# A graph transformer kernel on one core: seven edge buffers of seven slots with even chunks, four node blocks ahead of the type sort, single blocks and a third product tile at the end of the first layer

## Chip, cores and metric

The kernel runs on one core of a Trainium2 chip. The metric is the device time of one execution in microseconds (us), lower is better. The core has a matrix engine (TensorE, PE in the profile), a vector engine (VectorE, DVE), a scalar engine (ScalarE, ACT) and GpSimd (POOL), which here issues every indirect transfer, that is, every gather and scatter with addresses from a list. SyncE (SP) issues plain transfers; 16 DMA engines move the data.

## The reference

6250 nodes of 128 features, 100,000 edges sorted by destination, 16 node types and 32 edge types, 8 heads of 16, everything in float32. Two layers, then a linear layer and a layer norm:

```python
def gt_layer(x, ntype, etype, src, dst, Wk, Wq, Wv, Wa, Watt, Wmsg, pri, skip, g, b):
    k = typed_linear(x, ntype, Wk).reshape(n, H, HS)    # a weight matrix per node type
    q = typed_linear(x, ntype, Wq).reshape(n, H, HS)
    v = typed_linear(x, ntype, Wv).reshape(n, H, HS)
    kT = jnp.einsum('nhd,htdo->nhto', k, Watt)          # every node with every edge type
    vT = jnp.einsum('nhd,htdo->nhto', v, Wmsg)
    kw = kT[src, :, etype]
    m = vT[src, :, etype]
    a = jnp.einsum('ehd,ehd->eh', kw, q[dst]) * pri[:, etype].T / SQRT_D
    att = edge_softmax(a, dst, n)
    msg = (m * att[:, :, None]).reshape(-1, H * HS)
    hag = jax.ops.segment_sum(msg, dst, num_segments=n)
    h = jax.nn.silu(typed_linear(hag, ntype, Wa))
    alpha = jax.nn.sigmoid(skip[ntype])[:, None]
    h = h * alpha + x * (1.0 - alpha)
    return layernorm(h) * g + b
...
return layernorm(x + (layer1(layer0(x)) @ ff_w + ff_b))
```

## The kernel before

**The table.** Each layer first makes, for every node, `kT` and `vT` with all 32 edge types and writes them to memory as a table: a row of 1 KB (128 numbers of K, 128 of V) for each pair of node and edge type. A node's 32 rows are written as two pieces of 16. `table_block` (L337) makes the two pieces of a block of 128 nodes: matmuls of the node's K or V with the block-diagonal edge weights `bdk`, `bdv` (L349) into PSUM tiles `tb`, copies of these (by ScalarE L357, some by the vector engine L355) into a staging tile `st` of 2.1 MB, and then a store: one indirect DMA of GpSimd, L1163 for layer 0 and L1753 for layer 1.

**Start and first table.** `load_first` and its neighbours (L186 to L215, L374 to L385) load the weights. The edge weights come as eight strided transfers each for `Watt` and `Wmsg`, in runs of 64 bytes, into memory set to zero, and `scale_edge_weights` multiplies them by `pri`. Next the nodes are sorted by type: counts by matmul (L442 to L470), a place for each node, and three rounds (L483 to L493) of one-hot matrices and matmuls that turn places into the list `inv`, which says which node stands where. `fetch` (L508) gathers sorted node rows by `inv` (L515), `first0` and `linears0` make K and V of a type's blocks, and the loop at L1176 goes through 49 sorted blocks, two pieces each, 98 in all. Beside it the vector engine sorts the edges' destinations by degree (`ranking`), which decides the order of nodes in the edge stage. In this stretch the engines DVE and POOL run in program order.

**The edge stage** (`edges`, L1302, once a layer). The nodes are sorted by degree into blocks of 128, and each block has as many slots as the largest degree in it: `OWN_SLOTS` = 25, 21, 19, 18, ... slots for four groups of nodes with four node types each, and `MIXED_SLOTS` = 42, 20, 16, 14, 9 for nodes that don't fit. That makes 49 blocks and 819 slots. A slot is one gather of 128 table rows (L1519). The loop (L1485 to L1559) takes a block's slots in chunks of `CH` = 4: for each chunk a buffer `kv` (12 of them), its gathers, the product with the query (L1535) and the reduction to scores (L1541). After each of the three operations stands one `step()`, which advances the closing sequence of the block before (`finished`, L1362) by one step: mask, maximum, exponential, the products of V with the weights chunk by chunk, and the sums over slots. A buffer goes back to the gathers once its V product has been added up. The 42-slot block has 26 slots of its own and 2 more shared by a few nodes (`OWN`, `REST`): seven chunks and one for the rest. Between the chunks `tick` advances other work by a count of slots: the queries of the next superblock, the node chain (`nodes`, L1617: divide, typed linear, silu, mix, norm, and in layer 0 K, V and Q of layer 1), and in layer 0 the table pieces of layer 1 (`pieces_of`, L1765; scatters L1753). In layer 1 the chain ends in the row writes of the output (`put_out`, L1783). `leave` (L1336) counts chunks down and lets each such row write go after `7+2*i` chunks. Instructions recorded by the helper `on` all have line 267.

**The end of a layer.** The superblocks (up to four blocks each) are cut at L1225 to L1239. The last group's are laid out so that its final superblocks hold two blocks each, the last of all with 25 and 21 slots. The first gather of layer 1 waits for every piece of layer 1's table, so the last superblock's node chain and pieces stand between the layers. A product tile `tb` of layer 0's edge stage holds two banks; there are two such tiles, used in turn.

Of the kernel before, what the change touches and what calls it, by code (L numbers as in the profile page):

```python
# [10 lines left out]
F32 = mybir.dt.float32  # L11
BF16 = mybir.dt.bfloat16
# [8 lines left out]
P = 128  # L21

J = 17
# [10 lines left out]
CH = 4  # L34
# [19 lines left out]

def windows_of_types(n, pad, types, width):

    import math  # L60

    low, high = [0], [0]
    for t in range(1, types):
        share = t / types
        mean, dev = pad + n * share, math.sqrt(n * share * (1 - share))
        low.append(max(0, int((mean - 5.0 * dev) // P) * P))
        high.append(int(mean + 5.0 * dev) + 1)
    assert n / types + pad + 5.0 * math.sqrt(n / types) <= width
    return low, high
# [3 lines left out]
def kernel(  # L73
# [53 lines left out]
    LO, HI = windows_of_types(N, NP - N, TY, WIN)  # L127
    WC = max(HI[t] - LO[t] for t in range(TY)) + WIN
    WB = -(-WC // P)

# [40 lines left out]
    wq0 = wts.tile([P, TY, D], F32, name="wq0")  # L171
    wa = wts.tile([P, TY, D], F32, name="wa")

    bdk = wts.tile([P, RT, 2 * HS], F32, name="bdk")
    bdv = wts.tile([P, RT, 2 * HS], F32, name="bdv")
# [10 lines left out]
    def load_edge_weights(l):  # L186
        nc.vector.memset(bdk, 0.0)
        nc.vector.memset(bdv, 0.0)
        for h in range(H):
            s = slice(h * HS, (h + 1) * HS)  # L190
            c = slice((h % 2) * HS, (h % 2 + 1) * HS)
            nc.scalar.dma_start(bdk[s, :, c], Watt[l, h].rearrange("t d o -> d t o"))
            (nc.scalar if l else nc.sync).dma_start(bdv[s, :, c],
                                                    Wmsg[l, h].rearrange("t d o -> d t o"))
        (nc.scalar if l else nc.sync).dma_start(
            prit,
            pri[l].unsqueeze(1).to_broadcast([H, HS, RT]))

    def scale_edge_weights():

        first = nc.vector.tensor_scalar(prit, prit, 1.0 / float(HS) ** 0.5, None, op0=ALU.mult)
        nc.vector.tensor_tensor(bdk, bdk, prit.unsqueeze(2).to_broadcast([P, RT, 2 * HS]),
                                op=ALU.mult)
        return first
# [3 lines left out]
    def load_first():  # L208
        load_typed(wkqv[:, 0], Wk[0])
        load_typed(wkqv[:, 1], Wv[0])  # L210
        load_edge_weights(0)
# [125 lines left out]
    def table_block(pool, ps_pool, kT, vT, i, share, bufs, store, w=1):  # L337


        for tg in range(TG):  # L340
            tt = slice(tg * 16, (tg + 1) * 16)
            st = pool.tile([P, 16, 2 * D], F32, name="st", bufs=bufs)
            for half, (yT, bd) in enumerate(((kT, bdk), (vT, bdv))):
                for hp in range(0, HP, w):
                    pt = ps_pool.tile([P, w, SB * P], F32, name="tb").rearrange(
                        "p b (t c) -> p b t c", t=16)
# [27 lines left out]
    nc.sync.dma_start(ntr, ntype.rearrange("(i p) -> i p", p=P))  # L374
    nc.sync.dma_start(dsti, dst[0:P])
# [3 lines left out]
    nc.sync.dma_start(wq0, Wq[0].rearrange("t d o -> d t o"))  # L379
    nc.sync.dma_start(wa, Wa[0].rearrange("t d o -> d t o"))  # L380
# [3 lines left out]
        engines={mybir.EngineType.DVE, mybir.EngineType.Pool}))  # L384
# [14 lines left out]
    nc.gpsimd.iota(rowi, pattern=[[0, 1]], base=0, channel_multiplier=1)  # L399

# [4 lines left out]
    for t in range(TY):  # L405
        nc.gpsimd.memset(base_t[:, 0, t:t + 1], float(LO[t]))
        nc.gpsimd.memset(base_t[:, 1, t:t + 1], float(HI[t] - LO[t]))
# [34 lines left out]
    ty1 = tp.tile([P, TY, NT], BF16, name="ty1", tag="st", bufs=STB0)  # L442
    nc.vector.tensor_tensor(ty1, ntf.unsqueeze(1).to_broadcast([P, TY, NT]),
                            colf[:, :TY].unsqueeze(2).to_broadcast([P, TY, NT]), op=ALU.is_equal)
    ty1f = ty1.rearrange("p t i -> p (t i)")
    sums_t = tp.tile([P, 4, wide], F32, name="sums_t", tag="st", bufs=STB0)
    cnt_t, run_t, at_t, got_t = (sums_t[:, i] for i in range(4))
    ones = pp.tile([P, P], F32, name="ones")
# [7 lines left out]
    for m, pss in ((ones_b, c_pss), (upto_b, b_pss)):  # L456
        for h, ps in enumerate(pss):
            nc.tensor.matmul(ps[:, :half], m, ty1f[:, h * half:(h + 1) * half],
                             start=True, stop=True)
    nc.vector.tensor_copy(cnt_t[:, :half], c_pss[0][:, :half])  # L460
    nc.vector.tensor_copy(cnt_t[:, half:], c_pss[1][:, :half])
    nc.vector.tensor_tensor_scan(run_t, ones[:, 0:1].to_broadcast([P, wide]), cnt_t, 0.0,
# [4 lines left out]
    nc.vector.tensor_tensor(got_t, at_t, ty1f, op=ALU.mult)  # L467
    place = pp.tile([P, NT], F32, name="place")
# [3 lines left out]
    nc.vector.tensor_copy(placei, place)  # L472
# [7 lines left out]
    row1 = tp.tile([P, NT, P], BF16, name="row1", tag="st", bufs=STB0)  # L480
    col1 = tp.tile([P, NT, 2, NT], BF16, name="col1", tag="st", bufs=STB0)
    inv_ps = pps.tile([P, 2, NT], F32, name="ps")
    for i0 in range(0, NT, 17):  # L483
        sl = slice(i0, min(i0 + 17, NT))
        k = sl.stop - sl.start
        nc.vector.tensor_tensor(col1[:, sl, 1], placeb[:, sl].unsqueeze(2).to_broadcast([P, k, NT]),
                                colb[:, :NT].unsqueeze(1).to_broadcast([P, k, NT]), op=ALU.is_equal)
        nc.vector.tensor_tensor(col1[:, sl, 0], col1[:, sl, 1],
                                colb[:, sl].unsqueeze(2).to_broadcast([P, k, NT]), op=ALU.mult)
        nc.vector.tensor_scalar(col1[:, sl, 1], col1[:, sl, 1], rowf, None, op0=ALU.mult)  # L490
# [1464 lines left out]
```

## Time and profile before

| | us |
|---|---|
| median of 3 runs (2978.79 to 2982.26) | 2979.05 |
| profiled execution, its own time | 2978.13 |
| span of its profile | 2976.3 |
| start, up to the first table write | 53.45 |
| from there to the first gather of layer 0 | 540.3 |
| edges of layer 0, first to last gather | 1164.35 |
| between the layers, to the first gather of layer 1 | 86.77 |
| edges of layer 1, first to last gather | 1090.03 |
| from the last gather to the end | 41.44 |

The prediction quotes rows of the profile. In the rows of the windows view a window comes first, then its length and the busy time of each engine with the number of its instructions in parentheses (PE matmuls, PEld weight loads, DVE, ACT, POOL), the clock granted to TensorE as a share of full speed, the busy share of the 16 DMA engines, and the GB/s that they moved. A row of the groups has line, engine, operation, output<-inputs, count, then busy us and mean ns, then idle time of the engine just before these instructions and what ended most of it. A row of the timeline has start, duration, engine, line, operation, tiles, and in brackets the idle time before it and what ended it: "issue" is time in which the engine waited for nothing that the profile shows.

### The profile page before, as it was taken

What the parts mean: (1) busy time and instruction counts of PE and PEld (TensorE: products, weight loads), DVE (VectorE), ACT (ScalarE), POOL (GpSimd) and SP (SyncE); (2) the same over time, 40 slices, a digit from 0 to 9 for tenths busy, and PEclk for the clock granted to TensorE, in tenths of its full rate; (3) what the DMA queues carried; (4) which work ended last, traced back from release to release, by engine and by line L of the source; (5) the groups of instructions that cost most, each with busy time, mean ns of one, the idle gap of its engine ahead of it and who ended that gap; (6) DMA issues with size and microseconds to landing.
All of it is one profiled execution on the core that took longest, in us unless ns stands there. A gap on an engine that the chain in (4) does not pass through costs nothing. (4 is left out here: it accounts for less than half of the span.)

```text
span 2976.3 us, 21675 instructions
## 1 busy us (share of the span) xinstructions
PE 1670.6 (56%) x5325; PEld 727.2 (24%) x5325; DVE 1895.5 (64%) x4351; ACT 996.6 (33%) x1678; POOL 1975.7 (66%) x2116
## 2 busy tenths in 40 slices
PE   5999978523779887889788995022132113121212
PEld 2444434301323432333233332001011001000001
DVE  7567655357656767677666552576567667766665
ACT  3887533211434444435454562011111111111112
POOL 3332566377777777777777652777777777777773
PEclk9988866655777776787767665555555556555555
DMA  7999999953677678867788895333333333333331
GB/s 210 416 419 419 390 389 396 395 133 104 220 288 271 227 264 300 294 238 278 282 322 297 323 351 222 105 109 111 109 109 111 111 111 110 112 108 106 108 101 51
DMA packets 163487, 671.38 MB, mean 226 GB/s; under 512 B 52012, under 2 KB 78926, under 8 KB 138302
## 3 DMA queue, kind: packets, MB, share of 16 engines
q0 software_dynamic: 113152, 635.19, 59.5%
q1 hardware_dynamic: 34218, 27.57, 3.3%
q10 hardware_dynamic: 15976, 7.10, 1.0%
q8 instruction: 46, 0.75, 0.1%
q14 instruction: 95, 0.78, 0.1%
HBM read 245.42 MB, written 425.02 MB: 225 GB/s over the span
## 5 line engine op out<-in xcount | busy, mean ns | idle before, releaser
L1519 POOL DMA_INDIRECT kv<-tab,ell x1638 | 1566.8, 957 | 531.6 <-issue 422.5
L357 ACT COPY st<-tb 128x512 f32<-128x512 f32 (+1 forms) x984 | 687.5, 773 | 565.9 <-PE tb L349 405.2
L1535 DVE TENSOR_TENSOR kv<-kv,held 128x512 f32<-128x512 f32 (+3 forms) x446 | 284.9, 640 | 549.7 <-DMA kv<-tab,ell 459.5
L349 PE MATMUL tb<-bdk,kvT 32*128 32x512 f32 x784 | 295.9, 888 | 45.9 <-ACT st L357 45.7
L349 PE MATMUL tb<-bdv,kvT 32*128 32x512 f32 x784 | 286.3, 898 | 42.0 <-ACT st L357 41.6
L267 DVE TENSOR_TENSOR held<-kv,held 128x512 f32<-128x512 f32 (+3 forms) x444 | 287.2, 647 | 8.7
L349 PE MATMUL tb<-bdv,vT 32*128 32x512 f32 x784 | 261.8, 789 | 50.6 <-ACT st L357 46.5
L1541 DVE TENSOR_REDUCE a<-kv 128x32 f32<-128x512 f32 (+3 forms) x446 | 280.0, 632 | 0.9
L267 PE MATMUL nb<-by,all_rows 49*128 49x512 bf16 (+2 forms) x30 | 14.2, 475 | 402.4 <-DVE by L267 377.1
L267 PE MATMUL nb<-xm,wa 128*128 128x384 f32 (+2 forms) x336 | 185.7, 716 | 88.7 <-DVE xm L267 84.8
L1163 POOL DMA_INDIRECT tab<-st,rows x98 | 101.6, 1036 | 199.7 <-ACT st L357 167.7
L355 DVE COPY st<-tb 128x512 f32<-128x512 f32 (+1 forms) x192 | 128.9, 709 | 155.8 <-PE tb L349 87.0
L267 PE MATMUL nb<-xm,wkqv 128*128 128x384 f32 (+2 forms) x504 | 205.5, 562 | 10.2 <-DVE xm L267 10.2
L267 DVE TENSOR_TENSOR kv<-kv,held 128x512 f32<-128x512 f32 (+3 forms) x336 | 208.9, 622 | 2.2
L349 PE MATMUL tb<-bdk,kT 32*128 32x512 f32 x784 | 207.6, 790 | 2.4 <-issue 1.6
L267 PE MATMUL nb<-ident,hag 128*128 128x128 f32 x98 | 27.6, 424 | 296.8 <-DVE hag L267 296.8
L267 DVE SCALAR_TENSOR_TENSOR xm<-ntb,nb 128x512 f32<-128x512 bf16 (+2 forms) x304 | 157.3, 562 | 32.3 <-PE nb L267 30.1
L1753 POOL DMA_INDIRECT tab<-st,row x98 | 100.0, 1020 | 103.2 <-DVE st L355 37.1
L267 ACT ACTIVATE held<-a 128x128 f32<-128x128 f32 (+7 forms) x96 | 27.5, 287 | 325.9 <-DVE a L267 182.4
L267 PEld LDWEIGHTS nb<-xm,wa 128*128 128x128 f32 x336 | 88.7, 281 | 190.8 <-issue 79.0
L267 PEld LDWEIGHTS nb<-xm,wkqv 128*128 128x128 f32 x504 | 104.5, 216 | 121.7 <-issue 46.9
L349 PEld LDWEIGHTS tb<-bdv,vT 32*128 32x128 f32 x784 | 97.1, 228 | 148.4 <-ACT st L357 118.4
(342 smaller groups left out, 2094.8 us busy)
## 6 DMA issues: line engine op xcount, KB each, us to landing
kv<-tab,ell POOLq DMA_INDIRECT x1638
hq<-hqx SPq DMA_DIRECT2D x7, 768.0 KB, 5.5
hqx<-hs SPq DMA_DIRECT2D x7, 512.0 KB, 3.3
hq<-hqx SPq DMA_DIRECT2D x5, 576.0 KB, 3.8
hqx<-xr SPq DMA_DIRECT2D x10, 256.0 KB, 19.0
hqx<-hs SPq DMA_DIRECT2D x5, 384.0 KB, 3.1
hr<-hqx SPq DMA_DIRECT2D x7, 256.0 KB, 5.5
tab<-st,rows POOLq DMA_INDIRECT x98
```

The lines of the kernel that those rows point to most:

```text
L267: put = issue(*args, **kwargs)
L349: stream[nc.tensor] = nc.tensor.matmul(pt[:, b], yT[s, i * P:(i + 1) * P], bd[s, tt, :], start=True, stop=True)
L355: nc.vector.tensor_copy(to, pt)
L357: stream[nc.scalar] = nc.scalar.copy(to, pt)
L1163: put = nc.gpsimd.indirect_dma_start(out=tabs[0].rearrange("(n t) c -> n (t c)", t=16), out_offset=bass.IndirectOffsetOnAxis(ap=rows1[:, t ...
L1519: get = nc.gpsimd.indirect_dma_start(out=kv[:, j - j0, :], out_offset=None, in_=tabs[l][:], in_offset=bass.IndirectOffsetOnAxis(ap=ell[:, ...
L1535: stream[nc.vector] = nc.vector.tensor_tensor(kk, kk, of.unsqueeze(1).to_broadcast([P, c, D]), op=ALU.mult)
L1541: nc.vector.tensor_reduce(to, kk.rearrange("p k (h d) -> p k h d", h=H), axis=AX.X, op=ALU.add)
L1753: put = nc.gpsimd.indirect_dma_start(out=tabs[1].rearrange("(n t) c -> n (t c)", t=16), out_offset=bass.IndirectOffsetOnAxis(ap=row2[:, tg ...
```

## The change

1. *Edge buffers.* `CH` is 7, `kv` has 7 buffers (49 slots in place of 48), and a block's slots are divided evenly: 25 slots become four chunks, 21 to 15 three, 14 to 9 two, the own slots of the 42-slot block four. Five `step()` calls stand in a chunk. The sum of V products keeps four slots wide (`SUMS`). The output rows of layer 1 wait `4 + i` chunks.
2. *Blocks ahead of the sort.* On each partition the first node of each of the types 0 to 3 is taken: four blocks of one type each (`AHEAD`), known as soon as the type matrix is. Their rows are fetched, K and V made, and their eight pieces written between the steps of the sort (`beside_sort`). The sort leaves these nodes out, so 46 sorted blocks (`NS`) remain. The matrix and scalar engines too keep program order in this stretch. The sort's scratch lies in one tile, and the ahead pieces take their staging tiles in turn from two of the usual kind and the memory of `wq0` and `wa`, whose loads move behind the ahead pieces.
3. *Edge weights* come by two contiguous transfers, one row for each edge type, and 32 transposes and five vector operations spread them out in place of zeros, strided transfers and scaling. The K and V weights of the first four types are loaded first.
4. *End of layer 0.* The last group's final superblocks are one of two blocks and then two of one block, 25 slots and at last 21 (16 superblocks in place of 15). The last one's pieces use a third product tile, in the PSUM memory of `held`, and start as soon as K and V are there, ahead of the query part.

```diff
-CH = 4
+CH = 7
+SUMS = 4
...
+AHEAD = 4
...
-    def load_edge_weights(l):
-        nc.vector.memset(bdk, 0.0)
-        nc.vector.memset(bdv, 0.0)
-        for h in range(H):
...
+    def load_by_type(l, queue):
+        for i, w in enumerate((Watt, Wmsg)):
+            queue.dma_start(
+                by_type[i * RT:(i + 1) * RT].rearrange("t (h c) -> t h c", h=H),
+                w[l].rearrange("h t d e -> t h (d e)"))
+        queue.dma_start(prit, pri[l].unsqueeze(1).to_broadcast([H, HS, RT]))
+    def turned(ps):
+        for i in range(2):
+            for e in range(HS):
+                nc.tensor.transpose(
+                    ps[i][:, e * RT:(e + 1) * RT],
+                    by_type[i * RT:(i + 1) * RT].rearrange("t (c e) -> t c e", e=HS)[:, :, e],
+                    ident[i * RT:(i + 1) * RT, i * RT:(i + 1) * RT])
...
+    def spread_edge_weights(by_e):
+        nc.vector.tensor_scalar(prit, prit, 1.0 / float(HS) ** 0.5, None, op0=ALU.mult)
+        for a in range(2):
+            nc.vector.scalar_tensor_tensor(
+                bdk[:, :, a * HS:(a + 1) * HS], by_e[0], pair_of[:, a:a + 1],
+                prit.unsqueeze(2).to_broadcast([P, RT, HS]), op0=ALU.mult, op1=ALU.mult)
...
     def load_first():
-        load_typed(wkqv[:, 0], Wk[0])
-        load_typed(wkqv[:, 1], Wv[0])
-        load_edge_weights(0)
+        for t0, t1 in ((0, AHEAD), (AHEAD, TY)):
+            for i, w in enumerate((Wk, Wv)):
+                nc.scalar.dma_start(wkqv[:, i, t0:t1], w[0, t0:t1].rearrange("t d o -> d t o"))
...
+                    made[0] += 1
+                    pt = third if third is not None and made[0] % 3 == 0 else ps_pool.tile(
+                        [P, w, SB * P], F32, name="tb")
...
+    load_by_type(0, nc.sync)
...
-    nc.sync.dma_start(wq0, Wq[0].rearrange("t d o -> d t o"))
-    nc.sync.dma_start(wa, Wa[0].rearrange("t d o -> d t o"))
...
-        engines={mybir.EngineType.DVE, mybir.EngineType.Pool}))
+        engines={mybir.EngineType.Pool, *engines}))
...
+    nc.vector.tensor_tensor(toward, ty1[:, :AHEAD],
+                            toend.unsqueeze(1).to_broadcast([P, AHEAD, NT]), op=ALU.mult)
+    nc.vector.tensor_reduce(firstmost, toward, axis=AX.X, op=ALU.max)
+    nc.vector.tensor_scalar(ahead_f, firstmost, -float(P), rowend, op0=ALU.mult, op1=ALU.add)
+    nc.vector.tensor_scalar(ahead, ahead_f, float(NP - 1), None, op0=ALU.min)
+    for e in range(AHEAD):
+        nc.gpsimd.indirect_dma_start(
+            out=xa[:, e, :], out_offset=None, in_=x,
+            in_offset=bass.IndirectOffsetOnAxis(ap=ahead[:, e:e + 1], axis=0))
...
+    def ahead_steps():
+        yield from ahead_linears(hT, kT, vT, 0, 1)
+        rest = ahead_linears(hT, kT, vT, 1, AHEAD)
+        for _ in rest:
+            yield
+            break
+        for e in range(AHEAD):
+            def store(tg, st, e=e):
+                put0(st, ahead_rows[:, tg, e:e + 1])
+            for _ in table_block(tp, tnb, kT, vT, e, (), STB0, store, take=take):
+                next(rest, None)
+                yield
...
+    beside_sort(4)
+    spread_edge_weights(by_e)
+    beside_sort(3)
...
+        beside_sort()
...
+        for n, _ in enumerate(ahead_work):
+            stage = next(ranking, "done")
+            if n >= 5:
+                next(first, None)
+        for _ in first:
+            pass
+        nc.sync.dma_start(wq0, Wq[0].rearrange("t d o -> d t o"))
+        nc.sync.dma_start(wa, Wa[0].rearrange("t d o -> d t o"))
...
-                    cut += [(i0, 2) for i0 in range(SB - 2, -1, -2)]
+                    cut += [(2, 2)] + [(i0, 1) for i0 in range(2)]
...
-                acc = held[:, 0].rearrange("p (k c) -> p k c", k=CH)
+                acc = held[:, 0].rearrange("p (k c) -> p k c", k=SUMS)
...
-                    chunks = [(j, min(j + CH, own)) for j in range(0, own, CH)]
+                    many = -(-own // CH)
+                    cuts = [own * c // many for c in range(many + 1)]
+                    chunks = list(zip(cuts, cuts[1:]))
...
-                        kv = ep.tile([P, CH, 2 * D], F32, name="kv", bufs=12)
+                        kv = ep.tile([P, CH, 2 * D], F32, name="kv", bufs=7)
...
                         step()
+                        step()
...
+                        step()
                         step()
...
+                        if j == 1 and final:
+                            table(pieces_of(i0, k, outs[0], outs[1], True))
...
-                table(pieces_of(i0, k, outs[0], outs[1], (2,) if final else ()))
+                if not final:
+                    table(pieces_of(i0, k, outs[0], outs[1]))
...
-                    results.append([7 + 2 * i, (o, i0, i)])
+                    results.append([4 + i, (o, i0, i)])
...
+                yield from steps(table_block(ep, tps, kT, vT, i, (2,) if final else (), STB,
+                                             store, 2 if fast else 1,
+                                             third=held if final else None))
```

235 lines of the change are left out of this document (153 added, 82 removed).

## The prediction, made before the changed kernel ran

> **What bounds the kernel now.** I read the windows view first, cut at the program's own stages, then the groups of instructions, then GpSimd's timeline at the seams between stages.
>
> ```profile
> span 2976.3 us, 21675 instructions
> L1519 POOL DMA_INDIRECT kv<-tab,ell x1638 | 1566.8, 957 | 531.6 <-issue 422.5
> ...
> core 0: us, PE busy (x) PEld busy (x) DVE busy (x) ACT busy (x) POOL busy (x), PEclk, DMA share, GB/s
> 0.00:53.45 53.45, 19.79 (x92) 10.27 (x92) 36.30 (x109) 6.96 (x16) 16.81 (x70) 1.00 0.74 154
> 53.45:65.00 11.55, 8.51 (x42) 3.77 (x42) 8.57 (x30) 6.00 (x13) 3.09 (x5) 0.85 0.73 302
> 65.00:573.00 508.00, 450.20 (x1974) 217.26 (x1970) 300.74 (x674) 310.48 (x615) 238.39 (x257) 0.81 1.00 405
> 573.00:593.75 20.75, 0.00 (x0) 0.00 (x0) 0.06 (x1) 0.31 (x1) 0.97 (x1) 0.50 0.99 381
> ...
> 593.75:1758.10 1164.35, 906.86 (x2535) 355.99 (x2535) 778.91 (x1709) 480.34 (x675) 876.71 (x908) 0.71 0.74 260
> 1758.10:1844.87 86.77, 65.35 (x195) 26.83 (x192) 33.03 (x65) 36.53 (x50) 9.82 (x11) 0.61 0.70 279
> 1844.87:2934.90 1090.03, 211.11 (x473) 107.56 (x472) 716.01 (x1703) 147.85 (x298) 825.91 (x864) 0.54 0.37 109
> 2934.90:2976.34 41.44, 8.75 (x22) 5.48 (x22) 21.89 (x63) 8.14 (x13) 3.99 (x4) 0.54 0.04 12
> ```
>
> Five stages with different limits. From 65 to 593.75 us the 16 DMA engines are full (shares 1.00 and 0.99): the first table, 98 pieces of 2.1 MB, is written as fast as it can be. The two edge stages, 1164 and 1090 us, are GpSimd's, although its busy share reads only 0.75:
>
> ```profile
> 1876.57 0.95 POOL L1519 DMA_INDIRECT kv<-tab,ell  x1 [0.30 <-issue]
> 1877.82 0.95 POOL L1519 DMA_INDIRECT kv<-tab,ell  x1 [0.30 <-issue]
> ```
>
> One gather starts every 1.25 us, 0.30 of it unexplained issue. 819 gathers x 1.25 = 1024 us a layer; with 88 scatters of pieces between them in layer 0, and 47 row writes in layer 1, at about 1.3 us, that is 1138 and 1085 us out of 1164 and 1090. So work taken off the vector engine there gains nothing, and only a new wait of GpSimd costs. What can shrink is the start, the 86.8 us seam between the layers, and the 41 us tail.
>
> **The start.** The change takes, on each partition, the first node of types 0 to 3 as four ready blocks, and writes their tables before the sort is done.
>
> ```profile
> 4.08 0.97 DVE L443 TENSOR_TENSOR ty<-ntf,colf 128x784 bf16<-128x784 f32 x1
> 15.37 2.84 DVE L492 TENSOR_SCALAR row<-colb,placef 128x128 bf16<-128x128 bf16 x17
> 20.61 2.84 DVE L492 TENSOR_SCALAR row<-colb,placef 128x128 bf16<-128x128 bf16 x17
> 29.31 1.60 POOL L515 DMA_INDIRECT xg<-in_x_dram,inv  x1 [24.05 <-DVE inv L498]
> 53.45 1.02 POOL L1163 DMA_INDIRECT tab<-st,rows  x1 [0.30 <-issue]
> 67.03 7.99 ACT L357 COPY st<-tb 128x512 f32<-128x512 f32 x16
> 20.00:25.00 5.00, 2.86 (x17) 1.77 (x17) 4.93 (x21) 0.86 (x1) 0.00 (x0) 1.00 1.02 88
> ```
>
> Before, the first node rows are fetched at 29.31 and the first piece is written at 53.45, 24.1 us later. After, the index needs only the type matrix, done at 5.05, and four small vector operations: fetch at about 7. With the old 24.1 us the first write would come at 31; I estimate 25, as the fetch no longer queues behind the strided weight loads, but 32 transposes and five spreading operations come in between. That is 28 us earlier, and nearly all of it is worth nothing: the stage ends when the DMA engines have moved everything, so only idle DMA time and removed DMA work count. Idle before: 0.26 x 53.45 + 0.27 x 11.55 = 17.0 us. Idle after: about 2 at the start, 8 between the loads' end and the first write, and 6 more, since the next pieces' matmuls stand in program order behind the sort's rounds (one round every 20.61 - 15.37 = 5.24 us, two half-pieces each a round apart), while a piece is 5.2 us of DMA (2.1 MB at 405 GB/s). That is 16. The two query and output weights (2 MB) move from the start into the full stretch; they are work either way. Removed: the 16 strided loads of the edge weights, half a megabyte that ran at 88 GB/s, 6 us, against about 1.5 for the contiguous ones. So 17.0 - 16 + 4.5 = 5.5: **-6 us**, between 0 (idle grows as much as work shrinks) and -21 (no idle left). The extra vector work (some 6 us before the sort ends) is hidden by the ahead pieces; a piece's eight copies take 8 x 0.50 = 4.0 us on ScalarE alone, less than 5.2, so the full stretch stays full. There will be 100 pieces, but rows without a node are not written, so bytes stay.
>
> **Edge buffers.** Chunks per layer fall from 224 to 139, gathers stay 819. In layer 0 and 1 the vector engine loses 155 operations each (85 query products, 85 reductions, 37 value products less, 52 additions more).
>
> ```profile
> L1535 DVE TENSOR_TENSOR kv<-kv,held 128x512 f32<-128x512 f32 x183 | 125.7, 687 | 308.8 <-DMA kv<-tab,ell 293.2 <-issue 10.4 <-ACT held L1351 4.9
> L1535 DVE TENSOR_TENSOR kv<-kv,held 128x128 f32<-128x128 f32 x12 | 3.4, 284 | 8.9 <-DMA kv<-tab,ell 5.3 <-ACT held L1351 3.6
> 900.09 0.97 POOL L1519 DMA_INDIRECT kv<-tab,ell  x1 [2.19 <-DVE held L267]
> 2142.19 0.94 POOL L1519 DMA_INDIRECT kv<-tab,ell  x1 [1.52 <-DVE held L267]
> ```
>
> 128 to 512 elements cost 0.284 to 0.687, so 0.15 is fixed: 155 x 0.15 = 23 us a layer less busy, hidden behind the gathers. The cost is in the buffers. The 42-slot block takes 8 of 12 now (seven chunks and the rest); the 20-slot block behind it gets 4 chunks in before GpSimd must wait for the first buffer back, and it waits 2.19 and 1.52 us. After, it takes 5 of 7, and the next block's third chunk must wait. The buffer comes back in step 8 of the closing sequence: third chunk before (three steps a chunk), second chunk after (five). Before, GpSimd had one 4-slot chunk, 5.0 us, to issue past that point: the buffer came 7.2 and 6.5 us after. After, it has nothing to issue, and the operations ahead are longer (0.41 us for each 7-slot one, three of them): about 8.4 and 7.7. So +6.2 in each layer. Queued behind the waiting gather are all later gathers and scatters. A block of 25, 21 and 19 slots fills 4 + 3 buffers and has some 2 us left; with lag I put +1 on all of them. **+13 us**, from 0 (the closing sequence runs faster) to +40 (below).
>
> **The seam.** Before, the last superblock has two blocks, whose node chain and four pieces come after the last gather:
>
> ```profile
> 1758.09 0.98 POOL L1519 DMA_INDIRECT kv<-tab,ell  x1 [0.30 <-DVE held L267]
> 1780.02 0.69 DVE L267 TENSOR_REDUCE sums<-held 128x128 f32<-128x512 f32 x1
> 1787.20 0.69 PE L267 MATMUL nb<-ident,hag 128*128 128x128 f32 x2
> 1814.95 0.97 POOL L1753 DMA_INDIRECT tab<-st,row  x1 [25.35 <-DVE st L355]
> 1816.40 1.23 DVE L355 COPY st<-tb 128x1024 f32<-128x1024 f32 x1 [2.20 <-PE tb L349]
> 1835.53 0.97 POOL L1753 DMA_INDIRECT tab<-st,row  x1 [5.89 <-issue]
> 1844.87 0.99 POOL L1519 DMA_INDIRECT kv<-tab,ell  x1 [8.37 <-DMA tab<-st,row]
> 1820.00:1845.00 25.00, 13.96 (x33) 4.14 (x34) 5.95 (x5) 6.00 (x10) 3.05 (x4) 0.50 0.85 334
> ```
>
> The scatters are 6.86 us apart; the pieces take four of these, 27.4 us. Each product tile cycles in 1.23 (copy) + 2.20 (wait for the refill) = 3.43. After, one block is last: two pieces, eight tiles. With a third tile the refill runs beside the copy, so a pair costs about 2.4 in place of 3.43: 4 x 2.4 + 1.2 = 10.8. That saves 16.6. The chain ahead of it is shorter by about half of its matmuls, some 4 to 5 us (1787.20 to the first scatter was 27.8), and the pieces are started before the query part. Against it: two chains now, the 25-slot block's and the 21-slot block's, because the first one's sums stand behind the last chunk; they share ScalarE, TensorE and single buffers. I take 0 from that together. The landing of 8.4 us stays. **-21 us**, between -5 and -35.
>
> The granted clock in that stretch is 0.50 with TensorE busy 14 of 25 us. The Trainium skill, "TensorE: Matmul & The Clock Gate", section "HAM oscillation — how this bites in real kernels", says that idle gaps above about 3.4 us drop the array to half rate. By that rule denser tiles could restore the full clock, the refill would halve, and the seam would shrink by some 4 us more; the sum goes by the row.
>
> **The tail.**
>
> ```profile
> 2933.91 0.95 POOL L1519 DMA_INDIRECT kv<-tab,ell  x1 [0.30 <-issue]
> 2951.45 0.42 DVE L267 TENSOR_TENSOR hag<-sums,rd 128x256 f32<-128x256 f32 x1
> 2971.62 0.98 POOL L1785 DMA_INDIRECT out_dram<-o,node  x1 [0.30 <-issue]
> ```
>
> From the last gather to the last sums 17.5 us, then a two-block chain of 20.2. After: the last chunk has seven slots to process when it lands, and the other block's chain in between; the last chain has one block and takes about 14 to 15 (matmuls and row operations halve, waits stay). I estimate 17.5 + 2 + 15 against 37.7: **-3 us**, from -8 to +8.
>
> **Sum.** -6 + 13 - 21 - 3 = -17 on 2978.1, the profiled execution's own time (span 2976.3 and 1.8 around it): 2961. The median shown, 2979.05, is 0.9 above it: 2962.
>
> **Rivals.** *The vector engine's lag outgrows the buffers* (slower).
>
> ```profile
> 953.76 0.95 POOL L1519 DMA_INDIRECT kv<-tab,ell  x1 [0.30 <-issue]
> 974.06 0.88 DVE L1535 TENSOR_TENSOR kv<-kv,held 128x128 f32<-128x128 f32 x2 [1.43 <-ACT held L1351]
> ```
>
> In layer 0 the query product of a chunk gathered at 954.7 starts at 974.06: 19.4 us late. Twelve buffers swallow that. With seven, 3-chunk blocks leave about 12 slots (15 us) less the 6.5 us of the closing sequence: 8.5. Lag above 10 becomes a wait, of up to 9 us. Should layer 0 reach that five times, GpSimd waits some 35 us more: 2962 + 35 = 2997. For it: chains of a whole superblock now stand between fewer, longer chunks. Against: each wait lets the vector engine catch up, and it has 23 us less to do. 0.13. *Two chains in series* at both ends: 14 us added to seam and tail each, less what I had at zero: -6 + 13 - 8 + 7 = +6, 2985. 0.12. *All of it counts*: no idle DMA at the start (-20), clean seam (-33), small stalls (+5), tail -6: -54, 2925. 0.15. *The early tables do nothing*, as the DMA stretch ends where it did: 2968, inside the forecast.
>
> **Numbers.** Forecast (2940 to 2973) 0.60. Range 2928 to 2985. About 0.2%, 6 us, is what a measurement of this kernel can tell. Faster by more: 0.15 and nearly all of the forecast, 0.73. Within: the serial chains and the forecast's edge, 0.12. Slower: the lag and half of a serial case's upper side, 0.15.
>
> **What would show it.** First table write near 25 us, but the first gather no earlier than 575; gathers still 1.25 us apart; one wait of about 8 us per layer behind the 42-slot block; the seam at 60 to 70 us with the last scatters under 5.5 apart; tail near 38. Wrong: GpSimd waits of several us all through layer 0, a seam above 80, or a first gather before 570.

## The result, and the profile after

The changed kernel takes 3021.46 us (median of 3 runs, 3012.19 to 3025.66) against 2979.05: ratio 1.0137, 95% interval 1.0115 to 1.0158. It is slower, by 42 us or 1.4%; the forecast was 17 us faster.

The windows of the changed kernel, cut at the same seams as those of the kernel before:

```profile
span 3019.6 us, 21640 instructions
...
core 0: us, PE busy (x) PEld busy (x) DVE busy (x) ACT busy (x) POOL busy (x), PEclk, DMA share, GB/s
0.00:53.00 53.00, 33.28 (x187) 17.95 (x187) 45.31 (x147) 24.60 (x49) 21.68 (x75) 0.85 0.84 261
53.00:79.00 26.00, 19.41 (x97) 9.92 (x101) 5.53 (x23) 17.56 (x38) 6.15 (x8) 0.78 0.85 321
79.00:568.00 489.00, 433.55 (x1905) 206.88 (x1901) 291.44 (x652) 294.60 (x586) 235.06 (x255) 0.82 1.00 407
568.00:585.18 17.18, 0.00 (x0) 0.00 (x0) 0.45 (x2) 0.31 (x1) 0.27 (x2) 0.50 0.78 257
585.18:1786.40 1201.22, 932.29 (x2582) 365.77 (x2582) 773.60 (x1572) 480.82 (x680) 872.65 (x905) 0.70 0.71 250
1786.40:1875.67 89.27, 67.22 (x219) 29.59 (x217) 25.32 (x65) 43.64 (x62) 12.20 (x14) 0.61 0.74 293
1875.67:2975.00 1099.33, 211.53 (x470) 107.35 (x471) 704.24 (x1546) 146.94 (x296) 824.57 (x864) 0.54 0.37 108
2975.00:3019.60 44.60, 11.82 (x40) 8.43 (x38) 25.98 (x83) 15.84 (x25) 4.76 (x5) 0.50 0.05 14
```

By stage, each edge stage counted from the start of its first gather to the end of its last, all from the timelines:

| us | first gather | layer 0 | seam | layer 1 | tail | span |
|---|---|---|---|---|---|---|
| before | 593.8 | 1165.3 | 85.8 | 1090.0 | 41.5 | 2976.3 |
| after | 585.2 | 1202.9 | 87.6 | 1100.1 | 43.8 | 3019.6 |
| difference | -8.6 | +37.6 | +1.8 | +10.1 | +2.3 | +43.3 |
| forecast | -6 | +6.5 | -21 | +6.5 | -3 | -17 |

Layer 0 carries the loss. In GpSimd's timeline of the changed kernel the gathers still start 1.25 us apart, but the queue stops, above all at these places (the number in brackets is the idle time before the instruction; L1666 is the gather, L1906 the scatter of a piece):

```profile
883.85 1.01 POOL L1906 DMA_INDIRECT tab<-st,row  x1 [1.86 <-ACT st L383]
896.61 1.46 POOL L1666 DMA_INDIRECT kv<-tab,ell  x1 [11.76 <-DVE held L290]
...
1185.77 1.02 POOL L1906 DMA_INDIRECT tab<-st,row  x1 [6.78 <-ACT held L1495]
...
1335.12 1.01 POOL L1666 DMA_INDIRECT kv<-tab,ell  x1 [6.55 <-DVE held L290]
...
1540.24 1.02 POOL L1906 DMA_INDIRECT tab<-st,row  x1 [3.38 <-DMA kv<-tab,ell]
...
1724.87 1.02 POOL L1906 DMA_INDIRECT tab<-st,row  x1 [7.72 <-ACT st L383]
...
1756.83 1.01 POOL L1906 DMA_INDIRECT tab<-st,row  x1 [3.18 <-DMA tab<-st,row]
...
1778.27 1.01 POOL L1906 DMA_INDIRECT tab<-st,row  x1 [10.35 <-ACT st L383]
...
2179.19 1.41 POOL L1666 DMA_INDIRECT kv<-tab,ell  x1 [12.18 <-DVE held L290]
```

The two waits ahead of gathers at 896.61 and 2179.19 stand behind the 42-slot block, where the kernel before waited 2.19 and 1.52 us. The others are of two kinds: a gather that waits for a buffer, and a scatter that has come to the head of the queue before its piece is ready. All gathers behind such a scatter wait with it. By the profile, 19 of the 31.7 us of the scatters' waits end with ScalarE's copy of the piece (`st`), the rest with another ScalarE operation or a transfer. I added up the idle time beyond the usual 0.30 us, for gaps over 0.345 us:

| GpSimd's waits in layer 0, us | ahead of gathers | ahead of scatters | layer 1, gathers |
|---|---|---|---|
| before (12 buffers of 4) | 3.9 | 7.5 | 1.2 |
| after (7 of 7) | 21.6 | 31.7 | 11.9 |

The growth, 17.7 and 24.2, is more than the 37.6 by some 4 us; two scatters fewer (2.6 us) fall into the stage. So both kinds matter.

Beside the runs *e5* to *e8* and *e13* to *e18* the kernel before itself took 3460 to 3478 us, in place of 2977 to 2982 beside the others, for a reason that was not found; of these runs only the ratio to it is used, and of some the seam, not the lengths of the edge stages.

### The profile page after: what moved, and what is told of

The parts are those of the page before. It is cut to its first block, busy times and chain, and to the rows that moved or that the text cites. A ratio compares the mean times of both kernels' runs of the same rounds, so it can differ in the third digit from the quotient of the medians.

```text
span 3019.6 us, 21640 instructions
## 1 busy us (share of the span) xinstructions
PE 1709.1 (57%) x5492; PEld 745.9 (25%) x5492; DVE 1871.9 (62%) x4085; ACT 1024.3 (34%) x1734; POOL 1977.3 (65%) x2123
## 5 line engine op out<-in xcount | busy, mean ns | idle before, releaser
L1666 POOL DMA_INDIRECT kv<-tab,ell x1638 | 1564.6, 955 | 557.7 <-issue 459.8
L1682 DVE TENSOR_TENSOR kv<-kv,held 128x768 f32<-128x768 f32 (+2 forms) x276 | 259.8, 942 | 644.1 <-DMA kv<-tab,ell 505.8
L375 PE MATMUL tb<-bd,kvT 32*128 32x512 f32 x1560 | 538.7, 876 | 71.7 <-ACT st L383 71.0
L290 PE MATMUL nb<-xm,wqa 128*128 128x384 f32 (+3 forms) x528 | 276.4, 680 | 134.9 <-DVE xm L290 133.1
L375 PE MATMUL tb<-bd,vT 32*128 32x512 f32 x800 | 265.1, 775 | 53.6 <-ACT st L383 45.1
L1689 DVE TENSOR_REDUCE a<-kv 128x48 f32<-128x768 f32 (+2 forms) x276 | 256.0, 931 | 0.3
L375 PEld LDWEIGHTS tb<-bd,kvT 32*128 32x128 f32 x1560 | 151.7, 240 | 323.4 <-ACT st L383 244.7
L290 PE MATMUL nb<-xm,wkqv 128*128 128x384 f32 (+3 forms) x528 | 220.2, 576 | 16.6 <-DVE xm L290 16.4
L375 PE MATMUL tb<-bd,kT 32*128 32x512 f32 x800 | 206.4, 792 | 0.2 <-ACT kT L1304 0.2
L290 DVE SCALAR_TENSOR_TENSOR xm<-ntb,nb 128x512 f32<-128x512 bf16 (+3 forms) x320 | 160.2, 540 | 64.0 <-PE nb L290 60.7
L290 DVE TENSOR_TENSOR kv<-kv,held 128x768 f32<-128x768 f32 (+5 forms) x266 | 190.8, 745 | 2.8
L1906 POOL DMA_INDIRECT tab<-st,row x98 | 99.6, 1017 | 125.9 <-ACT st L383 66.5
## 6 DMA issues: line engine op xcount, KB each, us to landing
hqx<-xr SPq DMA_DIRECT2D x10, 256.0 KB, 17.5
```

Of the source, the lines that this page charges most:

```text
L290: put = issue(*args, **kwargs)
L375: stream[nc.tensor] = nc.tensor.matmul(pt[:, b], yT[s, i * P:(i + 1) * P], bd[s, tt, :], start=True, stop=True)
L1666: get = nc.gpsimd.indirect_dma_start(out=kv[:, j - j0, :], out_offset=None, in_=tabs[l][:], in_offset=bass.IndirectOffsetOnAxis(ap=ell[:, ...
L1682: stream[nc.vector] = nc.vector.tensor_tensor(kk, kk, of.unsqueeze(1).to_broadcast([P, c, D]), op=ALU.mult)
L1689: nc.vector.tensor_reduce(to, kk.rearrange("p k (h d) -> p k h d", h=H), axis=AX.X, op=ALU.add)
L1906: put = nc.gpsimd.indirect_dma_start(out=tabs[1].rearrange("(n t) c -> n (t c)", t=16), out_offset=bass.IndirectOffsetOnAxis(ap=row2[:, tg ...
```

## The experiments

**Buffers as before (e1) and two blocks last as before (e2), and both (e3).**

```diff
 e1: -CH = 7                                          +CH = 4
     -chunks = list(zip(cuts, cuts[1:]))              +chunks = [(j, min(j + CH, own)) ...]
     -name="kv", bufs=7)                              +name="kv", bufs=12)
     (three steps a chunk, results.append([7 + 2 * i, ...]))
 e2: -cut += [(2, 2)] + [(i0, 1) for i0 in range(2)]  +cut += [(i0, 2) for i0 in range(SB - 2, -1, -2)]
 e3: both
```

> The changed kernel with the edge buffers as before (chunks of 4 in 12 buffers, three steps a chunk, output rows after 7+2*i chunks); early blocks, edge weights, single last blocks and third tile stay. Theory A, the seven buffers with long chunks cause the waits behind the 42-slot block (about 10 us more in each layer) and the five waits inside layer 0 (about 22 us): layer 0 shrinks from 1203 to about 1171, layer 1 from 1100 to 1090, median about 2980. Theory B, the waits inside layer 0 come from elsewhere (another order on TensorE) and only the 42-slot block is the buffers' doing: layer 0 about 1193, median about 3001.

> The changed kernel with the last two blocks of layer 0 in one superblock again; the third product tile stays. Theory A, the single blocks cram the node chain and the pieces of the last superblocks into too few slots: the 12.8 us that the 25-slot block takes longer come back, and the seam falls from 87.6 to about 78 by the third tile alone, median about 2999. Theory B, the single blocks shorten the chain and the backlog comes from the long chunks: the last blocks stay as slow, the seam gets longer by about 10 us, median 3020 or more.

> Both undone: only the blocks ahead of the sort, the edge weights' loads and the third tile (with the early start of the last pieces) stay. Theory A: the start keeps its 8.6 us, the seam gains about 8, layers as before: median about 2962. Theory B, the start's gain is given back in layer 0: about 2971.

| | median us | ratio to before, interval | layer 0 | seam | layer 1 | tail |
|---|---|---|---|---|---|---|
| e1 | 2982.65 | 1.0020 (1.0008 to 1.0033) | 1167.1 | 90.6 | 1096.7 | 35.8 |
| e2 | 3006.28 | 1.0092 (1.0072 to 1.0113) | 1198.9 | 77.6 | 1100.0 | 43.7 |
| e3 | 2967.38 | 0.9962 (0.9951 to 0.9972) | 1168.2 | 78.4 | 1090.4 | 42.2 |

With the old buffers layer 0 is back at 1167 and 1168, against 1165.3 before: all but 2 to 3 us of that stage's loss belongs to the buffers, theory A. The runs undo them as a whole: length of the chunks, even cut, number of buffers and closing steps. Of the scatters' waits 14.3 us stay in both (7.5 before), so 6.8 of their growth of 24.2 is not the buffers'. The single blocks cost layer 0 4 us with the long chunks and nothing with the short ones, not the 12.8 that I had expected; but they lengthen the seam by 9.9 us (87.6 against 77.6) and 12.2 us (90.6 against 78.4). With both undone the rest of the change is worth 0.4%; 2967 lies between the 2962 and 2971 of e3's two theories. At the end of layer 1, e1 has a tail that is 6.3 us shorter than that of e3 and a layer 1 that is 6.3 us longer, so nothing is gained: a row write waits for its node chain ahead of the last gather.

```profile
2935.18 0.94 POOL L1663 DMA_INDIRECT kv<-tab,ell  x1 [0.30 <-issue]
2940.48 1.01 POOL L1934 DMA_INDIRECT out_dram<-o,node  x1 [4.36 <-DVE o L290]
2941.80 0.97 POOL L1663 DMA_INDIRECT kv<-tab,ell  x1 [0.30 <-issue]
```

**More closing steps behind the 42-slot block (e4).**

```diff
-                        step()
-                        step()
+                        for _ in range(8 if b == TOP + 1 and j0 == 0 else 2):
+                            step()
```

> The changed kernel with eight closing steps in place of two behind the first query product of the block that follows the 42-slot block. Theory A, the wait behind the 42-slot block is set by where the closing steps stand among the chunks: the two waits of 11.8 and 12.2 us fall below 4, median about 3005. Theory B, seven buffers are too few wherever the steps stand: waits stay above 8, median 3015 or more.

3010.68 us, ratio 1.0111 (1.0092 to 1.0129). The two waits halve, and neither theory has its number:

```profile
890.88 1.46 POOL L1666 DMA_INDIRECT kv<-tab,ell  x1 [6.18 <-DVE held L290]
...
2172.58 1.48 POOL L1666 DMA_INDIRECT kv<-tab,ell  x1 [6.45 <-DVE rs L290]
```

Where the steps stand sets about half of the wait; the other half was not taken apart. Layer 0 hardly gains by it (1200.1 against 1202.9): the gathers' waits fall by 6.3 us to 15.3, and the scatters' grow by 5.6 to 37.3. Layer 1, which has no such scatters, gains 5.4 us (1094.7).

**Scatters later (e9, at first e5), smaller chunks (e10, at first e6), fewer small buffers (e11, at first e7).** The first run of each, e5 to e7, had ratios of 1.0360, 1.0200 and 1.0157.

```diff
 e9 (on e2):  -late.append([8, (tg, st, b)])     +late.append([14, (tg, st, b)])
 e10 (on e2): -CH = 7, kv bufs=7                 +CH = 6, kv bufs=8
 e11 (on e3): -kv bufs=12, one step              +kv bufs=10, four steps in the first two chunks
                                                  behind the 42-slot block
```

> Scatters 14 steps behind their copies once more, two blocks last, because the runs before this one met a chip on which the kernel before itself took 3470 us, so that their stages can't be set beside the others. If the kernel before takes about 2977 here: theory A (a scatter waits because it stands too early in GpSimd's queue) gives a layer 0 of about 1178, theory B (GpSimd waits at the full buffers instead) above 1193. The ratio of 1.036 on the other chip speaks for B.

> Eight buffers of six slots, even chunks, two blocks last, once more. If the kernel before takes about 2977: theory A (losses grow with the length of a chunk and the scarcity of buffers) gives a layer 0 of about 1183 in place of 1199 and about 8 us behind the 42-slot block; theory B (any even cut with five steps loses as much) above 1195.

> Ten buffers of four slots with more closing steps behind the 42-slot block, once more. If the kernel before takes about 2977: theory A (the room beside the held buffers) gives a layer 0 of 1180 or more against 1168 with twelve, theory B (the length of the chunk) one within 5 of 1168.

| | median us | ratio, interval | layer 0 | waits of gathers | of scatters | layer 1, gathers |
|---|---|---|---|---|---|---|
| e2, 7 of 7 | 3006.28 | 1.0092 | 1198.9 | 22.5 | 27.9 | 11.8 |
| e9, later scatters | 3063.71 | 1.0276 (1.0260 to 1.0291) | 1243.8 | 91.6 | 2.9 | 11.9 |
| e10, 8 of 6 | 3017.81 | 1.0127 (1.0112 to 1.0143) | 1192.4 | 25.0 | 16.2 | 20.7 |
| e3, 12 of 4 | 2967.38 | 0.9962 | 1168.2 | 1.9 | 14.3 | 1.5 |
| e11, 10 of 4 | 3004.96 | 1.0077 (1.0062 to 1.0093) | 1195.1 | 28.5 | 12.0 | 19.4 |

Two buffers of four slots less cost layer 0 27 us, theory A. The extra steps of e11 are not the cause: e12 below has them with twelve buffers, and its layer 0 takes 1169.0 us, with 1.2 us of gather waits. The vector engine frees a buffer only when the closing sequence of its block has gone over it, and with ten there is less room for its lag. GpSimd's timeline of e11 shows these waits along the whole layer, at gathers now:

```profile
883.84 1.78 POOL L1663 DMA_INDIRECT kv<-tab,ell  x1 [6.14 <-DVE held L290]
...
1129.73 0.98 POOL L1663 DMA_INDIRECT kv<-tab,ell  x1 [4.58 <-DVE held L290]
...
1451.61 0.94 POOL L1663 DMA_INDIRECT kv<-tab,ell  x1 [6.30 <-DVE mv L290]
...
1766.65 0.98 POOL L1663 DMA_INDIRECT kv<-tab,ell  x1 [6.93 <-DVE held L290]
```

A buffer holds 819/224 = 3.66 slots on average before and 819/139 = 5.89 after, so 12 of them hold 43.9 slots, seven 41.2, ten of four 36.6, and eight of six (158 chunks) 41.5. The waits of the gathers in layer 0 follow this room roughly (43.9: 1.9; 41.5 and 41.2: 25.0 and 22.5; 36.6: 28.5), with extra steps in e11. In layer 1 they don't: there 41.5 slots wait 20.7 us and 41.2 only 11.8. The average hides the place behind the 42-slot block. Seven of seven leave two buffers there, which the even cut of the next block fills with 13 slots; eight of six leave two with 10, and twelve of four left four with 16. In e10 the gathers wait 16.7 and 13.1 us there, not the 8 of its theory A, and its layer 0 of 1192.4 lies between its two theories.

The waits of the scatters don't follow the room: they are 12.0 and 14.3 with chunks of four (7.5 before), 16.2 with six, 27.9 with seven. Theory A of e9, that they come from the scatter's place, is half true: moved back, they vanish, and 69 us more of gather waits take their place. Theory B is the nearer one, and even its price was too low.

**An eighth buffer of seven (e13 and e18, control e14), fourteen of four (e15).** The memory came from one copy less of old rows, queries and transposed V (`hr`, `q`, `kvT1`).

> The changed kernel with two blocks last in layer 0 and eight buffers of seven slots in place of seven; the 7 KB for it come from one copy less of the old rows, the queries and the transposed V. Even cuts and five steps stay, so 56 slots of memory hold about 47 in use. Theory A, what layer 0 lost is room beside the held buffers: it falls from 1199 to about 1175 and the waits behind the 42-slot block from 12 to about 3. Theory B, long chunks cost by their length: layer 0 stays above 1190.

> The control for it: the same copies less, but seven buffers. If the missing copies cost nothing, layer 0 takes 1199 and layer 1 1100 as with two blocks last; if they cost something, the difference is theirs and is taken off the run with eight.

> Chunks of four in fourteen buffers in place of twelve (early blocks and third tile stay, two blocks last, the same copies less). Theory A: with twelve only some 2 us in each layer were waits for a buffer, so fourteen save these and little more: layer 0 between 1160 and 1168, layer 1 about 1088. If the room were still scarce at twelve, layer 0 would fall below 1155.

> Two blocks last and eight buffers of seven slots once more (one copy less of old rows, queries and transposed V), because the earlier run met a chip on which the kernel before took 3478. If it takes about 2977 here: theory A (the loss of layer 0 is room beside the held buffers) gives 1175 in place of 1199 and waits of about 3 in place of 12 behind the 42-slot block; theory B (it is the length of the chunk) above 1190.

All four are among the runs of which only the ratio counts. Their ratios are 1.0252 (1.0214 to 1.0290) with eight, 1.0197 (1.0161 to 1.0232) for its control with seven, 1.0340 (1.0303 to 1.0376) with fourteen, and 1.0233 (1.0208 to 1.0259) with eight again. Against its control the eighth buffer gains nothing that these ratios show. No run has the copies less with twelve buffers, so the loss with fourteen can't be put to the buffers or to the copies. So neither theory is decided, and how much of the scatters' waits is the chunk's length by itself stays open too.

**The parts of the seam (e16, e17).** On e3, e16 gives the last pieces two product tiles in place of three, and e17 starts them behind the query part again.

```diff
 e16: -third=held if final else None))       +third=None))
 e17: -if j == 1 and final: table(...)       (the call stands behind q_rows again)
```

> Buffers and last superblock as before, early blocks kept, the last pieces started early but with the two product tiles of before. Theory A, the third tile brings the last four scatters from 6.9 to 3.9 us apart and that is most of the seam's gain: the seam grows from 78.4 back to about 85, median about 2974. Theory B, the gain comes from the early start of the pieces: the seam stays below 81.

> Buffers and last superblock as before, early blocks and the third product tile kept, but the last superblock's pieces start behind the query part again. In the runs with the early start the granted clock over the last pieces is 0.9 to 1.0 and a refill takes 1.23 us; before it was 0.50 and 2.20. Theory A, the early start keeps TensorE busy enough for the full clock: without it the clock is 0.50 again, the last four scatters lie 5 us or more apart and the seam grows from 78 to 84 or more. Theory B, the third tile does it: the clock stays above 0.9, the scatters 4 apart, and only the later start costs, seam 80 to 83.

The seam is 80.1 and 79.5 us. With both parts and chunks of four it is 77.9 and 77.8 in e8 and e15, and 78.4 and 77.6 in e3 and e12, so there it can be compared to about 1 us. With ten buffers it can't: the same kernel has 78.8 in e7 and 71.4 in e11. Windows over the last pieces: before, e3, e16 and e17.

```profile
1811.00:1836.50 25.50, 21.47 (x57) 6.47 (x54) 8.57 (x7) 7.08 (x7) 3.89 (x4) 0.50 0.63 255
```

```profile
1803.00:1819.50 16.50, 13.15 (x63) 4.40 (x60) 9.54 (x8) 8.11 (x10) 3.75 (x4) 0.99 0.69 285
```

```profile
2137.00:2157.50 20.50, 15.62 (x63) 5.20 (x64) 9.48 (x8) 8.25 (x10) 3.82 (x4) 0.89 0.74 303
```

```profile
2108.00:2124.00 16.00, 13.22 (x69) 5.50 (x67) 7.25 (x6) 6.78 (x9) 2.77 (x3) 1.00 0.44 180
```

The last column but two is the granted clock: 0.50 before, 0.99 with both parts, 0.89 and 1.00 with either alone. The numbers of theory B come out in both runs, though one names the early start and the other the third tile as the owner. No run leaves out both parts and keeps the rest of the change, so something that e3, e16 and e17 share may raise the clock as well; neither part is its sole owner.

GpSimd's timeline shows where the seam's gain of 7.4 us (85.8 to 78.4) lies, and what ends it. The first and the last of e3's four final scatters, and the first gather of layer 1:

```profile
1806.89 0.97 POOL L1901 DMA_INDIRECT tab<-st,row  x1 [21.11 <-DVE st L381]
...
1818.67 0.97 POOL L1901 DMA_INDIRECT tab<-st,row  x1 [2.48 <-issue]
1832.43 0.99 POOL L1663 DMA_INDIRECT kv<-tab,ell  x1 [12.78 <-DMA tab<-st,row]
```

From the last gather to the first of these scatters it is 56.9 us before, 53.8 in e3, 53.9 in e16 and 56.0 in e17, so the early start brings them 2 to 3 us forward. From there to the first gather it is 29.9, 25.5, 27.3 and 24.5. The scatters themselves lie 11.78 us from first to last in e3 in place of 20.58, 8.8 less, but half of that is lost again behind them: the wait for the landing grows from 8.37 to 12.78. From 1810 to 1825 the DMA engines are full (share 0.99, at 405 GB/s), so faster pieces have little more to give there. The ratios of the whole, 0.9997 (0.9972 to 1.0022) and 1.0004 (0.9981 to 1.0027), can't tell 2 us apart.

**A version of the parts that pay (e12, at first e8).** On e3, single last blocks in layer 1 alone, its last rows written behind the last gather, and four closing steps in the first two chunks behind the 42-slot block.

```diff
+            if l:
+                i0, k, types = sbs.pop()
+                sbs.extend((i0 + i, 1, types) for i in range(k))
...
-                        leave()
+                        if s + 2 < len(sbs):
+                            leave()
```

> Buffers and the end of layer 0 as before, single last blocks in layer 1 alone with the last rows written behind the last gather, more closing steps behind the 42-slot block, early blocks and third tile as changed, once more. If the kernel before takes about 2977: theory A 2958, theory B (the last chain is as long with one block as with two) 2963 or more.

2965.09 us, ratio 0.9941 (0.9928 to 0.9955); e8, the same kernel, 0.9969 (0.9949 to 0.9988). It is faster than both kernels, by 0.6% against the one before. The waits behind the 42-slot block fall to 1.27 and 0.99 us, but the tail is 41.4, as theory B had it, though not for its reason. The last chain, from `hag` to its last output `o`, does shorten, from 18.2 to 15.6 us between the starts of these two operations, but it starts later: the vector engine's last `hag` comes 20.2 us after the start of the last gather in place of 17.5.

## Why the prediction was wrong, point by point

**The start: right.** The first table write is at 25.84 (forecast 25), and still the first gather comes only 8.6 us earlier (forecast 6, and none before 575). Idle DMA is 0.16 x 53 + 0.15 x 26 + 0.22 x 17.18 = 16.2 us, of which the last 3.8 stand at the end of the stage, where the forecast had none: at the start it is 12.4 in place of the 16 forecast. So idle time gives about 1 us of the 8.6. By the windows the same 225 MB moved in some 7.5 us less of busy DMA time, an estimate from shares and rates; the removed strided loads (forecast 4.5) would explain it, but no run takes them alone. The 28 us of head start are worth little, as forecast. In the runs below the first gather comes 4.5 to 10 us earlier than before.

**The buffers: the step that failed first.** The prediction had "+1" on all blocks but the 42-slot one, and left the lag of the vector engine to a rival of 0.13. Layer 0 lost 37.6 us, of which 9.6 stands behind the 42-slot block and the rest at other places. The rival's price, 35 us above the forecast, nearly fits (31.1 more in layer 0 and 3.6 in layer 1), but that is luck. It had meant five waits for buffers; outside the 42-slot block the gathers' waits grew by only 8.1 us. What the prediction had not priced at all, in the sum or in the rival, is the scatter that comes to the head of GpSimd's queue before its piece is ready: these waits grew by 24.2 us. What it had priced, the room for gathers beside held buffers, does cause waits of the gathers, as e11 beside e12 shows. Why the scatters' pieces are late with long chunks was not isolated; e9 shows that moving the scatters back trades their waits for larger ones of the gathers.

The saving of 155 vector operations a layer was mis-sized too. In the windows of the edge stages 137 and 157 are gone, but DVE's busy time falls only from 778.9 to 773.6 us and from 716.0 to 704.2, 5.3 and 11.8 in place of 23 each. The stages did not get shorter by it, as forecast.

**Behind the 42-slot block: right mechanism, too small.** I expected waits of 8.4 and 7.7; they are 11.76 and 12.18. The vector engine's timeline of the second one shows what the estimate left out:

```profile
2168.85 1.09 DVE L1682 TENSOR_TENSOR kv<-kv,held 128x896 f32<-128x896 f32 x1 [3.20 <-DMA kv<-tab,ell]
2169.85 0.86 DVE L290 SCALAR_TENSOR_TENSOR hs<-nb,alpha,hb 128x128 f32<-128x128 f32 x3
2170.63 0.67 DVE L290 BATCH_NORM_STATS2 bn<-hs 128x6 f32<-128x128 f32 x3
2171.22 0.30 DVE L290 BATCH_NORM_AGGREGATE mv<-bn 128x2 f32<-128x6 f32 x3
...
2172.28 0.50 DVE L290 TENSOR_TENSOR a<-a,m 128x336 f32<-128x336 f32 x1
2172.70 1.08 DVE L1689 TENSOR_REDUCE a<-kv 128x56 f32<-128x896 f32 x1
2174.88 0.76 DVE L290 TENSOR_REDUCE den<-a 128x8 f32<-128x336 f32 x1 [1.10 <-ACT a L290]
...
2178.83 0.95 DVE L290 TENSOR_TENSOR kv<-kv,a 128x768 f32<-128x768 f32 x1
```

The product at 2168.85 starts only once all seven gathers of its chunk have landed, 3.20 us after the vector engine was free. Only behind it come the closing steps that free a buffer, and between them the node chain, which `tick` hands out by slots: with a chunk of seven 2.3 slots' worth at a time. I had counted the steps but not what is poured in between. Moving the steps forward (e4) took off half of the wait; no run takes the chain away, so its share is not shown.

**The seam: one term right, one of the wrong sign.** I forecast 16.6 us less for the pieces and about 5 less for the chain. The last two scatters of the changed kernel:

```profile
1861.72 0.98 POOL L1906 DMA_INDIRECT tab<-st,row  x1 [14.49 <-DVE st L381]
1865.68 0.97 POOL L1906 DMA_INDIRECT tab<-st,row  x1 [2.99 <-ACT hb L290]
1875.67 0.99 POOL L1666 DMA_INDIRECT kv<-tab,ell  x1 [9.01 <-DMA tab<-st,row]
```

From the first to the last of the final superblock's scatters it is 3.96 us in place of 1835.53 - 1814.95 = 20.58: 16.6 less. That this is the forecast's 16.6 is luck: the forecast took four intervals of 6.86 down to 10.8, 5.4 for each of two pieces, and what was measured is three intervals of 6.86 against one of 3.96, with a refill that is faster at a higher clock (below). The wait for the landing stayed near 8.4, at 9.01. But from the last gather to the first of them it is 1861.72 - 1787.16 = 74.6 in place of 1814.95 - 1758.09 = 56.9, so 17.7 more. TensorE's timeline shows why:

```profile
1795.10 0.47 PE L290 MATMUL nb<-ident,hag 128*128 128x128 f32 x1
...
1831.23 0.47 PE L290 MATMUL nb<-ident,hag 128*128 128x128 f32 x1
```

The matmul of `hag` is the first of a node chain. The chain of the 25-slot block starts at 1795.10, and the one of the last block 36 us later, at 1831.23: two chains in series, the rival of 0.12, to which the forecast had given "0 from that together". Undone, 9.9 us (e2) or 12.2 (e3 against e1) come back, of the 14 that the rival had.

**The tail: wrong for the same reason.** Forecast -3, measured +2.3. The same cut of superblocks serves layer 1, and there too the chain of the 25-slot block stands ahead of the last one. The vector engine's first operation of each chain in the changed kernel:

```profile
2985.42 0.28 DVE L290 TENSOR_TENSOR hag<-sums,rd 128x128 f32<-128x128 f32 x1
2995.65 0.29 DVE L290 TENSOR_TENSOR hag<-sums,rd 128x128 f32<-128x128 f32 x1
```

The last one starts 20.8 us after the start of the last gather; before, with one chain for both blocks, it was 17.5, and the forecast had 19.5. Layer 1 and tail together take the same with one block at the end as with two: 1143.9 us against 1143.7 with long chunks (e2), 1132.6 with short ones either way (e1, e3).

**The sum.** Against the forecast the start is 2.6 us better, layer 0 31.1 worse, layer 1 3.6, the seam 22.8 and the tail 5.3: 60.2 in all, which takes 2962 to the 3021 measured. Layer 0 alone would have put it at 2993, beyond a range that ended at 2985, and the seam alone at that end. Two rivals that I had priced one at a time came together. Two of the prediction's signs of being wrong are there: waits of several us all through layer 0, and a seam above 80.

## What to carry to other kernels

Count a set of buffers by the slots that are in use while the slowest consumer still holds a block, not by its memory: here 49 slots in seven hold 41.2 on average and 48 in twelve 43.9, because the cut leaves them partly empty, and what is left beside the largest block counts most. Where one in-order queue carries gathers and scatters, look for each edit at what comes to the head of the queue before its input is made, since everything behind it stops. And two half-sized pieces of work at the end of a stage only shorten it if they can run beside each other; where one list hands them out, they stand in series.

## What the runs showed of the hardware

A refill of two banks was awaited 2.20 us at a granted clock of 0.50 (the row at 1816.40 in the prediction) and 1.23 us at 1.00, here in e16, with two product tiles as before:

```profile
2144.10 1.22 DVE L381 COPY st<-tb 128x1024 f32<-128x1024 f32 x1 [1.23 <-PE tb L375]
```

What sets that clock the runs don't show. Before, in windows of 5 us:

```profile
1800.00:1805.00 5.00, 5.00 (x16) 4.06 (x15) 0.18 (x1) 0.37 (x1) 0.00 (x0) 0.62 0.01 2
1805.00:1810.00 5.00, 4.44 (x20) 2.17 (x18) 0.45 (x1) 1.66 (x4) 0.00 (x0) 1.00 0.05 20
1810.00:1815.00 5.00, 3.74 (x14) 1.80 (x16) 2.00 (x2) 1.49 (x2) 0.05 (x1) 0.57 0.09 33
1815.00:1820.00 5.00, 4.24 (x14) 1.00 (x8) 1.40 (x2) 2.02 (x2) 0.93 (x1) 0.50 0.74 315
1820.00:1825.00 5.00, 4.93 (x14) 1.97 (x16) 2.28 (x2) 1.01 (x1) 0.97 (x1) 0.50 0.62 262
1825.00:1830.00 5.00, 5.00 (x16) 1.38 (x14) 1.22 (x1) 2.02 (x2) 0.97 (x1) 0.50 0.62 264
```

The clock had come up to 1.00 when the pieces began and fell to 0.50 within 5 us. By the Trainium skill, "TensorE: Matmul & The Clock Gate", section "HAM oscillation — how this bites in real kernels", gaps above about 3.4 us halve the rate. Here it fell without one: TensorE's longest idle stretch as the clock fell was 1.09 us, at 1810.53.

```profile
1808.30 1.13 PE L349 MATMUL tb<-bdk,kvT 32*128 32x512 f32 x6
1810.53 2.38 PE L349 MATMUL tb<-bdv,kvT 32*128 32x512 f32 x8 [1.09 <-ACT st L357]
```

Nor is such a stretch enough: one of 1.10 us in e16 left the clock at 1.00 for the next 12 us.

```profile
2137.67 1.43 PE L375 MATMUL tb<-bd,kvT 32*128 32x512 f32 x8 [1.10 <-ACT st L383]
```

The share of busy time doesn't explain it either. From 1820 to 1830 TensorE was busy 9.93 of 10 us, as the profile counts it, and the clock stayed at 0.50; over the last pieces the share is 84% before at 0.50, and 80% in e3, 76% in e16 and 83% in e17 at 0.99, 0.89 and 1.00.
